# Choosing tokens in two mixture-of-experts layers: chunk maxima, one exponential, a gather from the resident activations, and weights issued earlier

## The chip, the cores and the metric

The kernel runs on one core of one Trainium2 chip. The metric is the device time of a whole execution in microseconds; the time given for a kernel is the median of its runs. One execution was taken with the hardware profiler. In its answers PE is the matmul engine (TensorE), PEld its weight loads, DVE the vector engine, ACT the scalar engine, POOL the GpSimd engine and SP the engine that issues most DMAs. Each engine works through its own instructions in order.

## The reference

Four layers act on a tensor of 4 batches, 128 channels and 64 x 64 positions: a state-space convolution, a graph convolution, and two layers of attention followed by a mixture of experts, on 4096 tokens of 128 values per batch. The change is in what follows an attention, and that is, cut to what matters:

```python
# z = layernorm(t);  t: 4 batches x 4096 tokens x 128
logits = einsum('bsd,ed->bse', z, gate_w) + gate_b       # 64 experts
probs = softmax(logits, axis=1)                           # over the 4096 tokens
vals, idx = top_k(probs.transpose(0, 2, 1), 8)            # each expert chooses 8 tokens
gathered = take(z, idx)                                   # 8 x 64 tokens of a batch
pooled = einsum('bked,bke->bed', gathered, topv)          # weighted sum of the eight
h = gelu(pooled_and_1 @ weight1)                          # 64 experts: 129 -> 512
out = h_and_1 @ weight2                                   # 513 -> 128
t = t + scatter_add(idx, out * topv)                      # back to the chosen tokens
```

An expert thus needs, for each batch, the eight largest of 4096 logits, their softmax weights, the weighted sum of the eight normed tokens, and its answer goes back to the same eight tokens with the same weights.

## The kernel before

Layers 0 and 1 run together until about 3330 us. `layer1_end` then fills `X`, a tile of 128 partitions x 4 batches x 32 blocks x 128 values, which stays on the chip: a block is 128 tokens, one per partition. `attn2`, `ffn("L2_ffn")`, `attn3` and `ffn("L3_ffn", out)` work on `X` in place.

`ffn` goes over two pairs of batches, `p` = 0 and 1; the two batches of a pair (`r` = 0, 1) take 64 partitions each, since there are 64 experts. Its steps, with the names and lines of the profile:

- *Logits.* Tokens come in 8 chunks of 512 (`c`). `ln_stats` (L700 to L712) gives mean and reciprocal deviation for 16 blocks at once: bn_stats on DVE, a square root on ACT. For each block `normed` writes the normed tile `zf` on DVE (L716), PE transposes it (L1071, `ps_t`), the four transposes are copied out (L1073, `zTf`, on ACT for r = 0 and on DVE for r = 1), and a matmul with the gate weights (L1074) gives logits in PSUM, which ACT writes with the bias to `lg` (L1077), 128 x 4096 in the end. The normed tiles of a whole pair are kept in `zs`: 17 buffers of four blocks.
- *Choice.* DVE finds the eight largest of each row of 4096 (L1081), writes a copy `ch` in which they are replaced by a very negative number (L1083), and negates the largest (L1085). ACT takes the exponential of `lg` in place, with its row sum `den` (L1087), and of `ch` (L1088). DVE subtracts the two (L1091). What is left in `lg` is the unnormalised softmax weight at the chosen tokens and zero elsewhere.
- *Gather.* For each chunk PE transposes `lg` (L1098, `ps_rt`), ACT copies it out (L1100, `rt`), and eight matmuls against the kept normed tiles sum the chosen tokens (L1104, `ps_p`). DVE divides by `den` (L1109), PE transposes (L1111), DVE writes `pooled` (L1112).
- *Experts.* Sixteen groups of four experts. `load` issues a group's two weight transfers of 1 MB each on SP's queue (L1048, L1051) and a small one on ACT's (L1053), into a pool of two buffers. Matmuls (L1126, L1128), Gelu on ACT (L1133), transposes (L1136), copy on DVE (L1138), matmuls (L1141), and after each four groups L1146 to L1150.
- *Scatter.* Matmuls of `lg` with the experts' answers (L1175), added to `X` on DVE (L1180); in the last layer the sum is transposed back as well and goes to the output (L1187 to L1196).

In attention 2 the normed tile is written by ACT in a second form, one activation with scale and bias (L776, bias from L760); the change uses this form in `ffn` too.

What order the engines follow is not the program's own. A scheduler orders the instructions of all stages by priority (about the order of the program) and by its own estimate of when each could run, and hands each engine one list. So work of a stage can stand ahead of its place: in the order before, nearly all statistics of a stage's tokens (L700) stand in the attention before it, and the first two weight groups of each `ffn` stand as soon as their buffers are free.

Of the kernel before, what the change touches and what calls it, by code (L numbers as in the profile page):

```python
# [19 lines left out]
N = 4096  # L20
CH = 512
NCH = N // CH
NB = N // P
E = 64
HF = 512
TOPK = 8


def bc(ap, n):
# [4 lines left out]
def bc_last(ap, n):  # L34

    return ap.unsqueeze(len(ap.shape)).to_broadcast([*ap.shape, n])


class Net:
# [652 lines left out]
                        (nc.vector.tensor_copy if h else nc.scalar.copy)(self.X[:, b, k : k + 4, :], pt)  # L692


    def ln_stats(self, sp, b, j0, n):

        nc, X = self.nc, self.X
        st = sp.tile([P, n, 6], F32, tag="lnst", name="lnst")
        for j in range(n):
            nc.vector.bn_stats(st[:, j, :], X[:, b, j0 + j, :])  # L700
        nm = sp.tile([P, n], F32, tag="lnnm", name="lnnm")
        rs = sp.tile([P, n], F32, tag="lnrs", name="lnrs")
        d = sp.tile([P, n], F32, tag="lnd", name="lnd")

        nc.vector.tensor_tensor(nm, st[:, :, 1], st[:, :, 4], ALU.add)
        nc.vector.tensor_tensor(d, st[:, :, 1], st[:, :, 4], ALU.subtract)
        nc.vector.tensor_tensor(rs, st[:, :, 2], st[:, :, 5], ALU.add)
# [147 lines left out]
    def attn3(self):  # L855
# [11 lines left out]
        with ExitStack() as ctx:  # L867
# [132 lines left out]
            for s in range(n + 4):  # L1000
# [8 lines left out]
                if 0 <= s - 3 < n:  # L1009
                    put(s - 3)  # L1010

    def ffn(self, name, out=None):

        nc, tc, a, X = self.nc, self.tc, self.a, self.X
        EG = 4
        NG = E // EG
        M = 32  # L1020
        with ExitStack() as ctx:
            wp = ctx.enter_context(tc.tile_pool(name="fw", bufs=1))
            big = ctx.enter_context(tc.tile_pool(name="fb", bufs=2))
            tp = ctx.enter_context(tc.tile_pool(name="ft", bufs=4))
            sp = ctx.enter_context(tc.tile_pool(name="fs", bufs=4))
            ew = ctx.enter_context(tc.tile_pool(name="fe", bufs=2))
            ps = ctx.enter_context(tc.tile_pool(name="fps", bufs=2, space=PSUM))
            aps = ctx.enter_context(tc.tile_pool(name="fa", bufs=2, space=PSUM))

            gw = wp.tile([E, P], F32, tag="gw", name="gw")  # L1030
# [11 lines left out]
            nc.vector.memset(pooled[:, E * B :], 0.0)  # L1042
            weights = []

            def load(g):
                e0 = g * EG
                w1 = ew.tile([P, EG, HF], F32, tag="w1", name="w1")
                nc.sync.dma_start(w1, a[f"{name}_weight1"][e0 : e0 + EG, 0:C, :].rearrange("e d h -> d e h"))  # L1048

                w2 = ew.tile([P, EG, 4, P], F32, tag="w2", name="w2f")  # L1050
                nc.sync.dma_start(w2, a[f"{name}_weight2"][e0 : e0 + EG, 0:HF, :].rearrange("e (p c) o -> p e c o", c=4))  # L1051
                b1 = ew.tile([EG, HF], F32, tag="b1", name="b1")
                nc.scalar.dma_start(b1, a[f"{name}_weight1"][e0 : e0 + EG, C, :])  # L1053
                return w1, w2, b1

            route, dens = [], []
            for p in range(B // 2):
                lg = big.tile([P, N], F32, tag="lg", name="lg")
                zs = [[big.tile([P, 4, P], F32, tag="z", name="zf", bufs=17) for r in range(2)] for c in range(NCH)]
                for c in range(NCH):  # L1060
                    pl = ps.tile([P, CH], F32, tag="ps", name="ps_l")
                    for r in range(2):
                        if c % 4 == 0:
                            if r == 0:
                                st = {}
                            st[r] = self.ln_stats(sp, 2 * p + r, 4 * c, 16)
                        pt = ps.tile([P, 4, P], F32, tag="tr", name="ps_t")
                        for i in range(4):
                            j = 4 * c + i
                            self.normed(zs[c][r][:, i, :], 2 * p + r, j, *st[r], j % 16)  # L1070
                            nc.tensor.transpose(pt[:, i, :], zs[c][r][:, i, :], self.ident)  # L1071
                        zT = tp.tile([P, 4, P], F32, tag="s", name="zTf")
                        (nc.vector.tensor_copy if r else nc.scalar.copy)(zT, pt)  # L1073
                        nc.tensor.matmul(  # L1074
                            pl[r * E : (r + 1) * E, :], gwT, zT.rearrange("p i c -> p (i c)"), start=True, stop=True
                        )
                    nc.scalar.activation(lg[:, c * CH : (c + 1) * CH], pl, AF.Identity, bias=gb)  # L1077


                m8 = sp.tile([P, TOPK], F32, tag="m8", name="m8")  # L1080
                nc.vector.max(m8, lg)  # L1081
                ch = wp.tile([P, N], F32, tag="ch", name="ch")
                nc.vector.match_replace(ch, m8, lg, -3.0e38)  # L1083
                nmax = sp.tile([P, 1], F32, tag="nmax", name="nmax")
                nc.vector.tensor_scalar(nmax, m8[:, 0:1], -1.0, None, ALU.mult)  # L1085
                den = sp.tile([P, 1], F32, tag="den", name="den")
                nc.scalar.activation(lg, lg, AF.Exp, bias=nmax, accum_out=den)  # L1087
                nc.scalar.activation(ch, ch, AF.Exp, bias=nmax)  # L1088
                nc.vector.reciprocal(den, den)

                nc.vector.tensor_tensor(lg, lg, ch, ALU.subtract)  # L1091
                route.append(lg)
                dens.append(den)
                pp = aps.tile([P, P], F32, tag="acc", name="ps_p")
                for c in range(NCH):
                    pt = ps.tile([P, 4, P], F32, tag="tr", name="ps_rt")
                    for i in range(4):
                        nc.tensor.transpose(pt[:, i, :], lg[:, (4 * c + i) * P : (4 * c + i + 1) * P], self.ident)  # L1098
                    rt = tp.tile([P, 4, P], F32, tag="s", name="rt")
                    nc.scalar.copy(rt, pt)  # L1100
                    for i in range(4):
                        j = 4 * c + i
                        for r in range(2):
                            nc.tensor.matmul(  # L1104
                                pp[r * E : (r + 1) * E, :], rt[:, i, r * E : (r + 1) * E], zs[c][r][:, i, :],
                                start=j == 0, stop=j == NB - 1,
                            )
                pd = tp.tile([P, P], F32, tag="s2", name="pd", bufs=3)
                nc.vector.tensor_scalar(pd, pp, den, None, ALU.mult)  # L1109
                pt = ps.tile([P, P], F32, tag="tr", name="ps_pt")  # L1110
                nc.tensor.transpose(pt, pd, self.ident)  # L1111
                nc.vector.tensor_copy(  # L1112
                    pooled[:, : E * B].rearrange("p (e b) -> p e b", b=B)[:, :, 2 * p : 2 * p + 2],
                    pt.rearrange("p (r e) -> p e r", r=2),
                )


            sel = self.sel
            outT = wp.tile([P, B, E], F32, tag="outT", name="outT")
            for q in range(NG // 4):  # L1120
                po = aps.tile([P, 4, P], F32, tag="acc", name="ps_eo")
                for k in range(4):
# [24 lines left out]
                pt = ps.tile([P, 4, P], F32, tag="tr", name="ps_oT")  # L1147
# [8 lines left out]
            for p in range(B // 2):  # L1156
                pt = ps.tile([P, P], F32, tag="tr", name="ps_ot")
# [9 lines left out]
            for p in range(B // 2):  # L1167
                for c in range(NCH):
                    for r in range(2):
                        if out is None:  # L1170

                            j = 4 * c + 2 * r
# [8 lines left out]
                        else:  # L1181

                            b = 2 * p + r
                            sl = slice(c * CH, (c + 1) * CH)
# [9 lines left out]
                            o = tp.tile([P, CH], F32, tag="s", name="of")  # L1194
# [16 lines left out]

# [47 lines left out]
```

## Time and profile before

| | us |
|---|---|
| median of three runs | 4361.5 (4350.91 to 4377.3) |
| profiled execution | 4357.93 |
| its span | 4356.1 |
| FFN 2: X final to the last logits of pair 1 | 97.3 (3661.2 to 3758.5) |
| FFN 2: from there to the first expert matmul L1128 | 38.05 |
| FFN 3: the same two stretches | 93.1 and 39.2 |
| layer1_end, attention 2, FFN 2 | 3330 to 3396, to 3661, to 3919 |
| attention 3, FFN 3 with the output | 3919 to 4066, to 4356 |

The span is what the profiler saw from the first instruction to the last; the profiled execution's own time is 1.8 us longer, and the median lies 3.6 above that. Stage bounds are rounded to a microsecond, as neighbouring stages overlap. In an answer about groups or the timeline a row gives a line, an engine and an operation with its output and inputs; a bracket holds the engine's idle time ahead of it and what ended that. Shares of busy time over the whole span (PE 82%, DVE 69%, ACT 48%) are averages over stages with different limits.

### The profile page before, as it was taken

What the parts mean: (1) busy time and instruction counts of PE and PEld (TensorE: products, weight loads), DVE (VectorE), ACT (ScalarE), POOL (GpSimd) and SP (SyncE); (2) the same over time, 40 slices, a digit from 0 to 9 for tenths busy, and PEclk for the clock granted to TensorE, in tenths of its full rate; (3) what the DMA queues carried; (4) which work ended last, traced back from release to release, by engine and by line L of the source; (5) the groups of instructions that cost most, each with busy time, mean ns of one, the idle gap of its engine ahead of it and who ended that gap; (6) DMA issues with size and microseconds to landing.
All of it is one profiled execution on the core that took longest, in us unless ns stands there. A gap on an engine that the chain in (4) does not pass through costs nothing. (4 is left out here: it accounts for less than half of the span.)

```text
span 4356.1 us, 49147 instructions
## 1 busy us (share of the span) xinstructions
PE 3553.7 (82%) x17367; PEld 1989.9 (46%) x17367; DVE 3002.4 (69%) x4815; ACT 2084.0 (48%) x3467; POOL 2463.4 (57%) x1235
## 2 busy tenths in 40 slices
PE   6877868888896888889688888989997798688768
PEld 2333333444543344554334445445654576347535
DVE  5988889897667999866699876655311776438721
ACT  4555654455544445654444555411322785308421
POOL 5999888887786988778698877820002100003100
PEclk8988978899998899999879999999997899799888
DMA  3454544555373444436445553631225100170045
GB/s 105 149 152 147 149 109 131 134 137 137 100 217 113 131 138 136 137 105 210 122 123 135 139 141 105 186 106 60 77 75 200 37 1 2 41 271 2 2 154 195
DMA packets 261991, 523.95 MB, mean 120 GB/s; under 512 B 22346, under 2 KB 24562, under 8 KB 261746
## 3 DMA queue, kind: packets, MB, share of 16 engines
q1 hardware_dynamic: 250450, 501.45, 39.2%
q10 hardware_dynamic: 11296, 19.37, 1.3%
q8 instruction: 137, 2.24, 0.2%
q14 instruction: 108, 0.88, 0.1%
HBM read 443.15 MB, written 77.59 MB: 120 GB/s over the span
## 5 line engine op out<-in xcount | busy, mean ns | idle before, releaser
L284 POOL TENSOR_TENSOR db<-dx,bt 128x1024 f32<-128x1024 f32 x512 | 1203.6, 2354 | 331.8 <-DVE hs L302 216.0
L302 DVE TENSOR_TENSOR_SCAN hs<-hs,carry,db 128x512 f32<-128x512 f32 x812 | 1035.2, 1282 | 176.0 <-ACT hs L296 93.5
L296 ACT ACTIVATE hs<-dl,A 128x512 f32<-128x512 f32 x1024 | 706.6, 692 | 744.6 <-DVE ho L312 691.0
L319 POOL TENSOR_TENSOR ho_s<-ho_s,ho 128x1024 f32<-128x1024 f32 x288 | 677.4, 2352 | 13.6 <-DVE ho L312 12.9
L497 PE MATMUL ps_g<-xn 128*128 128x512 f32 x1152 | 604.2, 655 | 98.5 <-DVE inc L500 73.1
L312 DVE TENSOR_TENSOR ho<-hs,bt 128x1024 f32<-128x1024 f32 x464 | 563.2, 1214 | 1.6
L520 PE MATMUL ps_ed<-xs,inc 128*128 128x258 f16 x4096 | 511.4, 285 | 19.5 <-DVE inc L500 8.7
L520 PEld LDWEIGHTS <-inc 128*128 128x128 fp8e4 x4096 | 416.6, 102 | 134.9 <-issue 62.1
L500 DVE SCALAR_TENSOR_TENSOR inc<-ps_g,hcl,hb 128x512 fp8e4<-128x512 f32 x576 | 420.3, 736 | 39.1 <-PE ps_g L497 23.2
L497 PEld LDWEIGHTS ps_g<-xn 128*128 128x128 f32 x1152 | 216.5, 205 | 416.3 <-DVE inc L500 182.3
L340 PE MATMUL ps_y<-ho,cst 128*128 128x512 f32 x512 | 275.1, 681 | 109.3 <-POOL ho L308 92.0
L620 PE MATMUL ps_v<-inc_v,es 128*128 128x512 fp8e4 x1536 | 342.6, 382 | 19.3 <-DVE rb L628 18.1
L620 PEld LDWEIGHTS <-es 128*128 128x128 f16 x2048 | 202.4, 99 | 288.5 <-issue 63.1
L513 ACT CAST inc<-ps_t 128x512 fp8e4<-128x512 f32 x448 | 232.1, 600 | 95.4 <-PE ps_t L509 95.3
L222 PE MATMUL ps_c<-xt,wc 128*128 128x512 f32 x512 | 234.0, 611 | 11.6 <-DVE inc L500 6.8
L340 PEld LDWEIGHTS ps_y<-ho,cst 128*128 128x128 f32 x512 | 105.5, 215 | 269.8 <-POOL ho L308 122.4
L526 ACT COPY ed<-ps_ed 128x129 f32<-128x129 f32 x128 | 34.0, 266 | 380.0 <-PE ps_ed L520 380.0
L527 DVE TENSOR_TENSOR ed<-ps_ed,ed 128x129 f32<-128x129 f32 x128 | 36.6, 286 | 211.1 <-ACT ed L526 208.1
L302 DVE TENSOR_TENSOR_SCAN hs<-hs,db 128x512 f32<-128x512 f32 x116 | 141.2, 1223 | 53.2 <-POOL db L284 42.2
L536 POOL TENSOR_TENSOR ed<-ed,rdeg 128x512 f32<-128x512 f32 x32 | 33.3, 1040 | 250.7 <-DVE rdeg L532 250.7
L222 PEld LDWEIGHTS ps_c<-xt,wc 128*128 128x128 f32 x512 | 99.2, 197 | 137.6 <-issue 116.4
L509 PE MATMUL ps_t<-ident,strip 128*128 128x128 fp8e4 x1344 | 114.8, 227 | 53.5 <-DVE ed L527 18.9
(293 smaller groups left out, 5513.2 us busy)
## 6 DMA issues: line engine op xcount, KB each, us to landing
bt<-bcd SPq DMA_DIRECT2D x512, 512.0 KB
inc<-inc SPq DMA_DIRECT2D x192, 256.0 KB
inc_v<-inc SPq DMA_DIRECT2D x96, 512.0 KB
w<-in_L_ffn_weight SPq DMA_DIRECT2D x32, 1024.0 KB
w2f<-in_L_ffn_weight SPq DMA_DIRECT2D x32, 1024.0 KB
strip<-inc SPq DMA_DIRECT2D x84, 256.0 KB
x<-x ACTq DMA_DIRECT2D x32, 256.0 KB
xn<-x SPq DMA_DIRECT2D x32, 256.0 KB
```

The costliest lines, as they stand in the source:

```text
L222: nc.tensor.matmul(s["ps"][h], wc[:, h, j, :], xt[:, j : j + T], start=j == 0, stop=j == 3)
L284: nc.gpsimd.tensor_tensor(db, s["dx"], bc(s["bt", n][:, 0, :], 2), ALU.mult)
L296: act(nc.scalar.activation(hs[:, k, :], s["dl"][:, k, :], AF.Exp, scale=A[:, k, n : n + 1]))
L302: nc.vector.tensor_tensor_scan(to[:, h, :], hs[:, h, :], db[:, h, :], init, ALU.mult, ALU.add)
L312: nc.vector.tensor_tensor(ho, hs, ct, ALU.mult)
L319: nc.gpsimd.tensor_tensor(s["sum", n // G], s["sum", n // G], ho, ALU.add)
L340: nc.tensor.matmul(s["y"][h], self.ident, t[:, h, :], start=False, stop=n == DS - 1 and k == len(terms) - 1,)
L497: nc.tensor.matmul(pq, xn[v // 4][:, v % 4 * P : (v % 4 + 1) * P], xn[c], start=True, stop=True)
L500: nc.vector.scalar_tensor_tensor(inc[:, v, :], pq, hc[:, v : v + 1], hb, ALU.subtract, ALU.is_gt, saturate=False)
L513: later(1, lambda: act(nc.scalar.copy(inc[:, v, :], pt, saturate=False)))
L520: nc.tensor.matmul(pe[:, : 2 * P + 2], inc[:, v, i * P : (i + 1) * P], xs[:, v, :], start=v == 0, stop=v == NB - 1,)
L620: nc.tensor.matmul(pv, es[:, e, k, :], inc[:, e, :], start=e == 0 and k == 0, stop=e == NB - 1 and k == 1,)
```

## The change

It changes `ffn` and what is issued ahead of it.

- The eight largest are found per chunk of 512, as its logits come (`best`, 8 x 8 per row), and then among these 64. The replacement writes -2^127. One exponential goes to a tile of its own, `ex`, and no longer to `lg`. An operation in four quarters of 1024 writes to `lg` the product of (`ch` = -2^127) and `ex`, in place of the second exponential and the subtraction.
- The normed tiles are not kept. `zf` has 8 buffers of one block; even blocks are written by DVE, odd ones by ACT. The reciprocal deviations of a pair are kept in `rsk`. The gather multiplies the transposed weights by them as it takes them out of PSUM, on DVE, sums over `X` itself, and takes off the mean with a row sum (`m`).
- The order in the program is logits(0), choose(0), logits(1), gather(0), choose(1), gather(1). The pool of two PSUM buffers has three.
- `load` becomes a method with a pool that lives for the whole kernel; groups 0 and 1 of layer 2 are issued ahead of attention 2, those of layer 3 ahead of attention 3. In the scheduled order, layer 2's now stand on SP's queue in layers 0 and 1 (near 2860 us by their neighbours), where they stood among the loads of `layer1_end`; layer 3's stand where they did.

The core of the diff; a line of "..." marks what is left out:

```diff
+TAKEN = -(2.0**127)
+EG = 4
...
-        rs = sp.tile([P, n], F32, tag="lnrs", name="lnrs")
+        if rs is None:
+            rs = sp.tile([P, n], F32, tag="lnrs", name="lnrs")
...
+    def load(self, name, g):
...
-            ew = ctx.enter_context(tc.tile_pool(name="fe", bufs=2))
-            ps = ctx.enter_context(tc.tile_pool(name="fps", bufs=2, space=PSUM))
+            ps = ctx.enter_context(tc.tile_pool(name="fps", bufs=3, space=PSUM))
...
-            def load(g):
...
+            rsk = [wp.tile([P, NB, 2], F32, tag=f"rs{p}", name="rsk") for p in range(B // 2)]
+            route, tops, dens = [], [], []
+            def logits(p):
                 lg = big.tile([P, N], F32, tag="lg", name="lg")
-                zs = [[big.tile([P, 4, P], F32, tag="z", name="zf", bufs=17) for r in range(2)] for c in range(NCH)]
+                best = sp.tile([P, NCH, TOPK], F32, tag="best", name="best")
+                st = {}
                 for c in range(NCH):
                     pl = ps.tile([P, CH], F32, tag="ps", name="ps_l")
                     for r in range(2):
                         if c % 4 == 0:
-                            if r == 0:
-                                st = {}
-                            st[r] = self.ln_stats(sp, 2 * p + r, 4 * c, 16)
+                            st[r] = self.ln_stats(sp, 2 * p + r, 4 * c, 16, rsk[p][:, 4 * c : 4 * c + 16, r])
+                            nm, rs = st[r]
+                            nb = sp.tile([P, 16], F32, tag="lnnb", name="lnnb")
+                            nc.vector.tensor_tensor(nb, nm, rs, ALU.mult)
+                            st[r] = nm, rs, nb
+                        nm, rs, nb = st[r]
                         pt = ps.tile([P, 4, P], F32, tag="tr", name="ps_t")
                         for i in range(4):
                             j = 4 * c + i
-                            self.normed(zs[c][r][:, i, :], 2 * p + r, j, *st[r], j % 16)
-                            nc.tensor.transpose(pt[:, i, :], zs[c][r][:, i, :], self.ident)
+                            z = tp.tile([P, P], F32, tag="z", name="zf", bufs=8)
+                            if i % 2:
+                                k = j % 16
+                                nc.scalar.activation(
+                                    z, X[:, 2 * p + r, j, :], AF.Identity, scale=rs[:, k : k + 1], bias=nb[:, k : k + 1]
+                                )
+                            else:
+                                self.normed(z, 2 * p + r, j, nm, rs, j % 16)
+                            nc.tensor.transpose(pt[:, i, :], z, self.ident)
                         zT = tp.tile([P, 4, P], F32, tag="s", name="zTf")
                         (nc.vector.tensor_copy if r else nc.scalar.copy)(zT, pt)
                         nc.tensor.matmul(
                             pl[r * E : (r + 1) * E, :], gwT, zT.rearrange("p i c -> p (i c)"), start=True, stop=True
                         )
                     nc.scalar.activation(lg[:, c * CH : (c + 1) * CH], pl, AF.Identity, bias=gb)
+                    nc.vector.max(best[:, c, :], lg[:, c * CH : (c + 1) * CH])
+                route.append(lg)
+                tops.append(best)
+            def choose(p):
+                lg = route[p]
                 m8 = sp.tile([P, TOPK], F32, tag="m8", name="m8")
-                nc.vector.max(m8, lg)
-                ch = wp.tile([P, N], F32, tag="ch", name="ch")
-                nc.vector.match_replace(ch, m8, lg, -3.0e38)
+                nc.vector.max(m8, tops[p].rearrange("p c k -> p (c k)"))
                 nmax = sp.tile([P, 1], F32, tag="nmax", name="nmax")
                 nc.vector.tensor_scalar(nmax, m8[:, 0:1], -1.0, None, ALU.mult)
+                ch = wp.tile([P, N], F32, tag="ch", name="ch")
+                nc.vector.match_replace(ch, m8, lg, TAKEN)
                 den = sp.tile([P, 1], F32, tag="den", name="den")
-                nc.scalar.activation(lg, lg, AF.Exp, bias=nmax, accum_out=den)
-                nc.scalar.activation(ch, ch, AF.Exp, bias=nmax)
+                ex = wp.tile([P, N], F32, tag="ex", name="exf")
+                nc.scalar.activation(ex, lg, AF.Exp, bias=nmax, accum_out=den)
+                for q in range(4):
+                    sl = slice(q * N // 4, (q + 1) * N // 4)
+                    nc.vector.scalar_tensor_tensor(lg[:, sl], ch[:, sl], TAKEN, ex[:, sl], ALU.is_equal, ALU.mult)
                 nc.vector.reciprocal(den, den)
-                nc.vector.tensor_tensor(lg, lg, ch, ALU.subtract)
-                route.append(lg)
                 dens.append(den)
+            def gather(p):
+                lg = route[p]
                 pp = aps.tile([P, P], F32, tag="acc", name="ps_p")
...
-                    nc.scalar.copy(rt, pt)
+                    nc.vector.tensor_tensor(
+                        rt.rearrange("p i (r e) -> p i r e", r=2), pt.rearrange("p i (r e) -> p i r e", r=2),
+                        bc_last(rsk[p][:, 4 * c : 4 * c + 4, :], E), ALU.mult,
+                    )
...
                             nc.tensor.matmul(
-                                pp[r * E : (r + 1) * E, :], rt[:, i, r * E : (r + 1) * E], zs[c][r][:, i, :],
+                                pp[r * E : (r + 1) * E, :], rt[:, i, r * E : (r + 1) * E], X[:, 2 * p + r, j, :],
                                 start=j == 0, stop=j == NB - 1,
                             )
+                m = sp.tile([P, 1], F32, tag="m", name="m")
+                nc.vector.reduce_sum(m, pp, axis=AX.X)
+                nc.vector.tensor_scalar(m, m, -1.0 / C, None, ALU.mult)
                 pd = tp.tile([P, P], F32, tag="s2", name="pd", bufs=3)
-                nc.vector.tensor_scalar(pd, pp, den, None, ALU.mult)
+                nc.vector.tensor_scalar(pd, pp, m, dens[p], ALU.add, ALU.mult)
                 pt = ps.tile([P, P], F32, tag="tr", name="ps_pt")
...
+            logits(0)
+            choose(0)
+            logits(1)
+            gather(0)
+            choose(1)
+            gather(1)
...
-                    w1, w2, b1 = load(g)
+                    w1, w2, b1 = self.ahead[g] if g < len(self.ahead) else self.load(name, g)
...
+    net.ew = ctx.enter_context(tc.tile_pool(name="fe", bufs=2))
     net.layer1_end()
+    net.ahead = [net.load("L2_ffn", g) for g in range(2)]
     net.attn2()
     net.ffn("L2_ffn")
+    net.ahead = [net.load("L3_ffn", g) for g in range(2)]
     net.attn3()
     net.ffn("L3_ffn", out)
```

More of the change, by code (lines that the diff above doesn't have):

```diff
@@ L692, in layer1_end, with ln_stats @@
                         (nc.vector.tensor_copy if h else nc.scalar.copy)(self.X[:, b, k : k + 4, :], pt)
-    def ln_stats(self, sp, b, j0, n):
+    def ln_stats(self, sp, b, j0, n, rs=None):
         nc, X = self.nc, self.X
@@ L1010, in attn3 @@
                     put(s - 3)
+    def load(self, name, g):
+        nc, a, ew = self.nc, self.a, self.ew
+        e0 = g * EG
+        w1 = ew.tile([P, EG, HF], F32, tag="w1", name="w1")
+        nc.sync.dma_start(w1, a[f"{name}_weight1"][e0 : e0 + EG, 0:C, :].rearrange("e d h -> d e h"))
+        w2 = ew.tile([P, EG, 4, P], F32, tag="w2", name="w2f")
+        nc.sync.dma_start(w2, a[f"{name}_weight2"][e0 : e0 + EG, 0:HF, :].rearrange("e (p c) o -> p e c o", c=4))
+        b1 = ew.tile([EG, HF], F32, tag="b1", name="b1")
+        nc.scalar.dma_start(b1, a[f"{name}_weight1"][e0 : e0 + EG, C, :])
+        return w1, w2, b1
     def ffn(self, name, out=None):
         nc, tc, a, X = self.nc, self.tc, self.a, self.X
-        EG = 4
         NG = E // EG
@@ L1043, in ffn @@
             weights = []
-            def load(g):
[L1046 to L1057, printed above, removed]
+            rsk = [wp.tile([P, NB, 2], F32, tag=f"rs{p}", name="rsk") for p in range(B // 2)]
+            route, tops, dens = [], [], []
+            def logits(p):
                 lg = big.tile([P, N], F32, tag="lg", name="lg")
-                zs = [[big.tile([P, 4, P], F32, tag="z", name="zf", bufs=17) for r in range(2)] for c in range(NCH)]
+                best = sp.tile([P, NCH, TOPK], F32, tag="best", name="best")
+                st = {}
                 for c in range(NCH):
```

## The prediction

> **What bounds the kernel now.** I read the granted clock first (mean 0.9, one core), then the slices, then the busy time stage by stage, because the change touches the two FFN stages and what is loaded for them. Stage times, in us from the span's start; columns: length, busy time of PE, weight load, DVE, ACT, POOL, granted clock, DMA share, GB/s.
>
> ```profile
> 3330.00:3396.00 66.00, 31.12 (x128) 24.93 (x128) 11.23 (x20) 29.74 (x34) 37.37 (x16) 0.53 0.78 271
> 3396.00:3661.00 265.00, 243.22 (x1652) 199.18 (x1651) 198.91 (x782) 207.42 (x446) 0.23 (x5) 0.97 0.01 2
> 3661.00:3697.00 36.00, 27.61 (x97) 11.38 (x97) 25.39 (x94) 11.79 (x20) 0.64 (x2) 0.86 0.02 3
> 3697.00:3718.00 21.00, 0.00 (x0) 0.00 (x0) 13.69 (x17) 10.27 (x6) 0.00 (x0) 0.55 0.00 0
> 3718.00:3758.00 40.00, 36.22 (x258) 22.81 (x259) 21.84 (x72) 13.69 (x24) 0.00 (x0) 0.94 0.00 1
> 3758.00:3781.00 23.00, 1.85 (x5) 0.48 (x4) 13.56 (x6) 9.18 (x5) 0.00 (x0) 0.56 0.00 1
> 3781.00:3797.00 16.00, 14.34 (x165) 12.06 (x169) 0.64 (x2) 4.39 (x8) 0.00 (x0) 0.89 0.01 2
> 3797.00:3884.00 87.00, 67.53 (x748) 31.96 (x740) 11.89 (x19) 13.07 (x21) 0.00 (x0) 0.88 0.91 340
> ```
>
> The rows are the end of layer 1, attention 2, and then FFN 2: logits of the first batch pair, its choice, gather with the second pair's logits, the second choice, gather, experts, scatter. In the two choice rows PE does nothing for 21 and 23 us; FFN 3 has two more (22 and 22 us). The experts' row is DMA's (share 0.91). The timeline gives the choice as one chain:
>
> ```profile
> 3695.77 4.43 DVE L1081 MAX8 m<-lg 128x8 f32<-128x4096 f32 x1 [0.86 <-ACT lg L1077]
> 3700.43 4.41 DVE L1083 MATCH_REPLACE8 ch<-m,lg 128x4096 f32<-128x4096 f32 x1
> 3704.98 1.28 ACT L1087 ACT_TABLE_LOAD   x1 [8.85 <-DVE nmax L1085]
> 3706.28 3.71 ACT L1087 ACTIVATE lg<-lg,nmax 128x4096 f32<-128x4096 f32 x1
> 3709.98 3.69 ACT L1088 ACTIVATE ch<-ch,nmax 128x4096 f32<-128x4096 f32 x1
> 3713.71 4.42 DVE L1091 TENSOR_TENSOR lg<-lg,ch 128x4096 f32<-128x4096 f32 x1 [3.44 <-ACT ch L1088]
> 3718.28 1.94 PE L1098 MATMUL ps_rt<-cst,lg 128*128 128x128 f32 x8 [23.26 <-DVE lg L1091]
> ```
>
> 4.43 + 4.41 + 1.28 + 3.71 + 3.69 + 4.42 = 21.9, plus hand-overs: PE stands 23.26 us. The waits of FFN 2 (waiter, releaser, total, times, longest) confirm it:
>
> ```profile
> PE ps_rt L1098 <- DVE lg L1091: 44.4, 2, 23.3
> ```
>
> In FFN 2 the last logits of pair 1 are there at 3758.5, 97.3 us after X is final (3661.2); the first expert matmul starts 38.05 us later (3796.56). In FFN 3: 93.1 and 39.2 us.
>
> [...] The trace shows 1.283 for the load, but the Exp starts 0.02 us after it[...]. [...] 0.55 in the choice row, and the first eight transposes take 1.94 us where eight at full clock take 1.09. [...]
>
> **The change, part by part** (new lines named by tile).
>
> *Logits.* Before, DVE writes all eight normed tiles of a chunk of 512 tokens and keeps them. Now DVE writes four, ACT four into eight short-lived buffers, and one maximum per chunk is added. DVE per chunk: 4 × 0.268 (L716 back to back) + one 128x512 copy 0.61 (L1073 overlapped) + maximum 0.6 (4.43/8 = 0.55 and a start; bounds 0.55 and 0.75) + about four bn_stats × 0.2 = 3.1. The bn_stats are new here: in the static order about 60 of an FFN's 128 stand in its logits phase, before nearly all were hoisted into attention. ACT: 4 × 0.40 to 0.50 (L776, the same operation, takes 0.496 alone) + copy 0.48 + lg 0.6 = 2.7 to 3.1. PE: 1.09 + 1.07 = 2.2. Before, pair 0's chunks took 3.6 us with DVE at 2.83, 79% of it. The same share of 3.1 gives 3.9; 3.3 would be DVE almost full. I take 3.8. Sixteen chunks: 60.8.
>
> *First choice.* It lies inside the logits: pair 1's follow in program order. DVE: match_replace 4.5, beside it the table load and one Exp (1.28 + 3.71 = 5.0), then four quarters of compare-and-multiply. A quarter has no row[...]. In all 4.5 + 0.6 + 4.9 = 10.0, in which PE gets only the tiles already queued.
>
> *Start.* In ACT's order five DMA issues, a Sqrt table load (1.28) and four small activations now stand ahead of its first normed tile. In FFN 2 I put the first transposes 7.2 us behind X, 4.3 in FFN 3 (the issues took to 3665.2 before); before, it was under 1.
>
> FFN 2: 7.2 + 60.8 + 10.0 = 78.0 for 97.3, −19.3. FFN 3: 75.1 for 93.1, −18.0.
>
> *Last logits to first expert matmul.* Maxima 0.75 and nmax 0.15, match_replace 4.5 (Exp hidden up to 0.6), rt of pair 0 six times between (6 × 0.69, DVE instead of ACT), four quarters 4.9: 14.5. These six rt and their matmuls are pair 0's gather, which fills PE where it stood 23 us. Then pair 1's gather: it took 3781.2 to 3796.6, 15.4 us, at the evacuation's 0.586 on ACT; at 0.69 on DVE with three PSUM buffers PE still sets it, 15.5 with the added row sum (0.3). Together 30, against 38.05 and 39.2: −8.0 and −9.2. A Gelu table load exposed before (1.28, ACT at 3797.7) is now ordered ahead; that is inside the 30.
>
> *Loads.* L2's first two groups (four of 1 MB) moved from among layer1_end's x loads to about 2860 us, behind three xn loads and ahead of the other stores and loads on SP's queue; two b1 loads move on ACT. DMA is at 0.49 in layers 0/1, and the next xn is wanted at 2887: 4.2 MB at 400 GB/s is 10.5 us, so 0 to +2, taken +1. In layer1_end DMA ran at 406 GB/s while the loads passed; tiles took 4.64 us, 3.87 after. Five tiles × 0.77 = 3.9 and a part of ACT's 7 us wait for x: −5 (bounds 0 and −13; nothing if POOL's 2.35 per tile or the rest of that pipeline takes over). L3's groups are issued where they were, behind L2's experts: 0.
>
> *Attention.* Fewer bn_stats inside it and table loads 22 to 14 in attention 2. PE holds the steady unit (7.51 us), units with loads take 8.0: four of them × 0.5 = −2 (−8 to +3). Attention 3 likewise −2.
>
> Sum: −37.3 − 17.2 − 5 − 4 + 1 = −62.5. The profiled execution took 4357.9 (span 4356.1): 4295.4. Median of the runs shown is 4361.5, 3.6 above it: 4299.
>
> **The rivals.**
> *Coupling (the other side).* Every transpose group now needs tiles of two in-order queues; a zTf or lg waiting for PE at ACT's head holds ACT's tiles, those hold the transposes, these the eight buffers DVE waits for. If each half chunk becomes a round trip, a chunk costs up to 2 × (z 0.5 + transposes 0.6 + copy 0.7 + matmul 0.55 + hand-overs 0.4) = 5.5. Break-even of an FFN: 16 × c + 17.2 − 8 = 97.3, c = 5.5; with the rest of −8 to help it is c = 5.75. At 6.2 the kernel takes about 4377. For: waits on both queues in the static order, 9.7 us ACT wait at L1073 in eight chunks already. Against: eight buffers are a whole chunk ahead, three PSUM buffers.
> *DVE becomes the bound.* With bn_stats, maxima, rt and hand-overs a chunk at 4.6: +0.8 × 32 = +26: 4325. For: DVE gains work just where it was 70% busy. Against: 3.1 summed.
> *Loading ahead is hidden or costs.* layer1_end limited by POOL and ACT, +5, and layers 0/1 +2: 4306.
> *Better overlap.* Chunks at 3.2, first choice half filled by queued work (−5 each): −19 − 10 = 4270.
> *That the choice doesn't shorten* is excluded: the removed Exp, maximum and whole-row subtract are on PE's wait itself, unless PE's filler order fails: then the tail is 38 again, 4316.
>
> **How the numbers follow.** Measurement tells about 0.5% (22 us) from no change. Forecast (with the loads' case) 0.58: 4282 to 4316. DVE bound or filler failing 0.22: 4316 to 4341. Better overlap 0.13: 4262 to 4282. Coupling 0.07: 4341 to 4390. The range, leaving out the tenth at either end: 4270 to 4336. Faster than 4340: 0.58 + 0.13 + 0.21 = 0.92; same 0.05; slower 0.03.
>
> **What would show it.** PE's wait for rt behind the choice below 12 us in the second choice, and gone as one block in the first; logits chunks at 3.8 (wrong if 4.5); last logits 78 and 75 us after X is final, the first expert matmul 30 later; granted clock in the FFN above 0.8 throughout; layer1_end at 61; experts unchanged at 87 and 99 us. Wrong if ACT's waits for ps_t and DVE's for zf's buffers grow beyond 1 us per chunk, if the experts' stage grows, or if X is final after 3661 (I expect 3655).

## The result

The changed kernel took 4333.65 us (median of seven runs, 4320.59 to 4347.82), the kernel before 4361.5 us (seven runs, 4350.91 to 4377.3). The ratio is 0.9933, 95% interval 0.9906 to 0.996: some 28 us gained, where 62.5 were forecast. The profiled execution took 4332.47 us, its span 4330.7, at a granted clock of 0.899 (0.900 before).

Stage times of the changed kernel, columns as in the prediction (length; busy time of PE, weight load, DVE, ACT, POOL; granted clock, DMA share, GB/s). The rows: end of layer 1, attention 2, FFN 2's logits of pair 0, from there to pair 1's last logits (the first choice is in it), from there to the first expert matmul, experts; then FFN 3's pair 0 and the stretch after it.

```profile
3339.00:3397.00 58.00, 29.48 (x120) 23.52 (x120) 10.37 (x15) 26.45 (x30) 37.08 (x16) 0.53 0.71 235
3397.00:3663.60 266.60, 246.65 (x1659) 201.18 (x1659) 186.43 (x704) 199.35 (x435) 0.40 (x6) 0.96 0.01 2
3669.30:3702.70 33.40, 28.72 (x103) 11.91 (x103) 25.59 (x95) 24.00 (x54) 0.00 (x0) 0.92 0.00 0
3702.70:3748.20 45.50, 32.40 (x110) 13.25 (x111) 34.82 (x95) 27.66 (x51) 0.00 (x0) 0.81 0.00 1
3748.20:3778.90 30.70, 26.20 (x316) 22.51 (x315) 21.08 (x32) 6.37 (x4) 0.00 (x0) 0.89 0.01 2
3778.90:3877.40 98.50, 77.27 (x751) 36.89 (x752) 14.43 (x28) 11.89 (x20) 0.00 (x0) 0.77 0.95 337
4055.80:4090.80 35.00, 28.01 (x99) 11.19 (x99) 26.70 (x102) 22.91 (x52) 0.00 (x0) 0.94 0.00 1
4090.80:4140.20 49.40, 35.63 (x113) 14.86 (x115) 35.72 (x98) 28.83 (x53) 0.00 (x0) 0.72 0.00 0
```

No engine is full in the logits: in pair 0 of FFN 2 DVE is in use for 25.6 of 33.4 us, ACT for 24.0. The choice itself is shorter, as its second instance shows in the timeline:

```profile
3748.17 0.69 DVE L1095 MAX8 best<-lg 128x8 f32<-128x512 f32 x1 [1.32 <-ACT lg L1094]
3748.90 0.23 DVE L1104 MAX8 m<-best 128x8 f32<-128x64 f32 x1
3749.30 4.41 DVE L1108 MATCH_REPLACE8 ch<-m,lg 128x4096 f32<-128x4096 f32 x1
3749.39 1.28 ACT L1111 ACT_TABLE_LOAD   x1 [1.25 <-DVE nmax L1106]
3750.69 3.71 ACT L1111 ACTIVATE exf<-lg,nmax 128x4096 f32<-128x4096 f32 x1
3754.36 5.39 PE L1136 MATMUL ps_p<-X,rt 128*64 128x128 f32 x48 [1.53 <-DVE rt L1129]
3755.42 3.49 DVE L1115 SCALAR_TENSOR_TENSOR lg<-ch,exf 128x1024 f32<-128x1024 f32 x3
```

Table load and Exp run beside match_replace, and pair 0's gather (L1136) fills PE. The wait of 23.26 us that carried the prediction is not among the waits of FFN 2 any more.

**Where the time went.** Executions of one kernel differ in two places that the change leaves nearly alone. The stretch up to layer1_end was between 3324.7 and 3340.9 us in all the profiles here, and an experts' stage between 90.9 and 108.5 where no work was added to it (the first experiment shows what its length goes with). Without these two, three profiles of the kernel before give 832.5, 831.2 and 830.8 us, two of the changed kernel 789.7 and 793.3: 40.0 us less. I take this for what the change does. The runs' 28 (17 to 41 by the interval) hold it together with those two, and 40 is near the end of that interval. But over the six variants below that have a ratio and leave the experts alone, the gain by the ratio less the gain outside the two places is between -8 and +12 us, and under 1 in the mean, so the runs don't show that the change costs time there. By stages, means of the same profiles:

| | before | after | change | forecast |
|---|---|---|---|---|
| layer1_end, first to last POOL add | 58.7 | 56.2 | -2.5 | -5 |
| attention 2 and 3 | 269.4, 146.6 | 268.6, 145.9 | -1.5 | -4 |
| FFN 2, X final to last logits | 95.6 | 85.8 | -9.8 | -19.3 |
| FFN 3, the same | 93.3 | 88.1 | -5.2 | -18.0 |
| last logits to first expert matmul | 38.8, 38.4 | 30.9, 30.9 | -15.4 | -17.2 |
| scatter of FFN 2, output of FFN 3 | 32.1, 58.5 | 29.0, 56.0 | -5.6 | 0 |

Of the 34 us by which the runs fell short of the forecast, 22 are one term, the logits: -15.0 where -37.3 was forecast. Most of what is left is the difference between 40 and 28.

### The profile page after: what moved, and what is told of

It is laid out like the page before. It is cut to its first block, busy times and chain, and to the rows that moved or that the text cites. A ratio compares the mean times of both kernels' runs of the same rounds, so it can differ in the third digit from the quotient of the medians.

```text
span 4330.7 us, 49179 instructions
## 1 busy us (share of the span) xinstructions
PE 3584.4 (83%) x17367; PEld 2004.0 (46%) x17367; DVE 3001.4 (69%) x4787; ACT 2094.7 (48%) x3551; POOL 2463.2 (57%) x1235
## 5 line engine op out<-in xcount | busy, mean ns | idle before, releaser
L304 DVE TENSOR_TENSOR_SCAN hs<-hs,db 128x512 f32<-128x512 f32 x116 | 141.3, 1223 | 54.3 <-POOL db L286 43.3
```

What stands on the lines that cost most here:

```text
L304: nc.vector.tensor_tensor_scan(to[:, h, :], hs[:, h, :], db[:, h, :], init, ALU.mult, ALU.add)
```

## The experiments

Ratios are to the kernel before on the same chip. "Pair 0" is from the first transpose to pair 0's last logits, "rest" from there to pair 1's, "tail" from there to the first expert matmul.

**Both kernels again.** No edit.

> The kernel before once more, for a second profile. If the clock of TensorE in the experts' stages is a matter of chance, the two stages (first expert matmul to the last ob) differ from 90.9 and 99.5 us by up to 8 us, with the time at half clock (21 and 38 us then), some 0.3 to 0.4 us for each us at half clock. If the change caused the 98.5 and 103.5 us of the kernel after, this one shows 91 and 99 again, within 2. Logits of pair 0: 34 and 31; from there to the last logits of pair 1: 63 and 62; tail 38 and 39.

> The changed kernel once more. Chance: experts' stages anywhere from 88 to 104 us, following the time at half clock. Caused by the change: 98.5 and 103.5 again within 2. The stretch up to the start of layer1_end was 5.8 us longer in its first profile, all of it gained before 1520 us, where nothing is changed: by chance it is within 6 us of 3333 again, with either sign; if the change did it, +5 to +6. Logits of pair 0: 33 and 35 with 5.7 and 3.7 of start; rest 45 and 49; tail 31.

> The kernel before a third time, for its experts' stages. Chance: FFN 2's and FFN 3's lie on the line of about 81 us + 0.4 x time at half clock, anywhere from 88 to 108, and one of the two FFN 2 stages so far (90.9, 93.9) could as well have been 100. If the change makes FFN 2's experts slower by itself, FFN 2's is 94 or less again, while the changed kernel and its variants had 95 to 107.

The kernel before had experts' stages of 93.9 and 108.5 us, and in a third profile 107.0 and 103.0; the changed one 101.8 and 107.4. So the kernel before, too, can have a long experts' stage in FFN 2, which speaks for chance and not for the change. Two executions of that one stage of the kernel before, first profile and third:

```profile
3796.60:3887.50 90.90, 69.70 (x754) 33.29 (x755) 14.44 (x28) 13.07 (x21) 0.00 (x0) 0.88 0.91 337
```

```profile
3786.80:3893.80 107.00, 86.19 (x753) 40.36 (x754) 14.44 (x28) 13.07 (x21) 0.00 (x0) 0.71 0.81 287
```

DVE's and ACT's work is the same to a hundredth; PE's is 16.5 us longer at a lower clock, and the DMA share falls with it. Over 30 experts' stages in 15 profiles (all but the variant with more PE work) the length is 86.4 us + 0.31 times the time at half clock, with a spread of 1.3 us about that line. Their mean is 100.5 in the kernel before (six) and 101.8 in the changed kernel and its variants (24).

The stretch up to layer1_end was 5.8 us longer in the changed kernel's first profile. Set side by side, POOL's instructions stand 5.7 or 5.8 us apart from 1837 us to 3333 us; the weight loads moved to 2866 add nothing to it. The step that was forecast at +1 is 0.

**Statistics left out.** Work is left out here (see the expectation).

```diff
-        for j in range(n):
+        for j in range(n if rs is None else 1):
             nc.vector.bn_stats(st[:, j, :], X[:, b, j0 + j, :])
+        if rs is not None:
+            nc.vector.tensor_copy(st[:, 1:, :], st[:, 0:1, :].to_broadcast([P, n - 1, 6]))
```

> Leaves work out: in the FFNs bn_stats runs for one block of 16 and its result is copied to the other 15; the output is not the reference's. It takes about 110 bn_stats of 0.27 us off DVE in each FFN, all else stays. If DVE's sum sets the chunks (3.2 us of 4.2 in use), pair 0's eight chunks fall from 33.4 and 35.0 to 26 to 28 us, the rest of the logits by 5 to 6 us each, the kernel by 24 us or more. If the hand-overs between the in-order queues set them, they stay within 2 us (31 to 35) and the kernel gains under 10 us, most of it in attention where some of these instructions stood.

```profile
3660.50:3693.60 33.10, 28.67 (x101) 11.40 (x101) 21.53 (x70) 23.57 (x55) 0.00 (x0) 0.93 0.00 0
3693.60:3735.90 42.30, 32.53 (x111) 12.73 (x113) 28.84 (x56) 26.43 (x49) 0.00 (x0) 0.88 0.00 1
```

DVE has 4.1 us less in pair 0, which stays at 33.1 (35.1 in FFN 3): DVE's sum doesn't set pair 0. The rest fell from 45.5 and 49.4 to 42.3 and 41.4, so there DVE's work does count. Outside layers 0/1 and the experts this variant took 775.6 us, 14 to 18 less than the changed kernel, which is between the two expectations. The ratio was 0.9891 (0.9867 to 0.9914).

Most of what the rest gained lies in one place. Statistics come for sixteen blocks, that is for four chunks, at a time. In the changed kernel those of pair 1's second half are finished only when its fifth chunk needs them:

```profile
3727.11 0.69 ACT L1094 ACTIVATE lg<-ps_l,gb 128x512 f32<-128x512 f32 x1 [0.69 <-PE ps_l L1091]
3728.94 1.44 DVE L702 BATCH_NORM_STATS2 lnst<-X 128x6 f32<-128x128 f32 x7
3731.20 0.31 ACT L714 ACTIVATE rsk<-rsk,eps 128x16 f32<-128x16 f32 x1 [0.60 <-DVE rsk L712]
3731.93 1.11 DVE L719 TENSOR_SCALAR zf<-X,lnnm,rsk 128x128 f32<-128x128 f32 x4
3736.31 0.69 ACT L1094 ACTIVATE lg<-ps_l,gb 128x512 f32<-128x512 f32 x1 [2.17 <-PE ps_l L1091]
```

The fifth chunk's logits came 9.2 us after the fourth's (8.8 in FFN 3); without the statistics it was 3.5 in both.

**All normed tiles on DVE.**

```diff
-                            if i % 2:
+                            if False:
```

> All normed tiles on DVE again, everything else as in the changed kernel. DVE gains 32 tiles x 0.31 = 10 us per pair. If DVE's sum sets the chunks, pair 0 goes from 33.4 and 35.0 to about 43 us, and the kernel is 25 to 40 us slower than the changed one. If the hand-overs between two engines that share each transpose group set them, pair 0 stays at 33 to 37 although DVE does 1.2 us more per chunk, and the kernel stays within 12 us of the changed one.

Pair 0 took 37.4 and 37.4 us, just above the second expectation, and the rest 59.6 and 62.0 us. Outside layers 0/1 and the experts it took 817.7 us, 24 to 28 more than the changed kernel, close to the first expectation; ratio 0.9983 (0.9966 to 1.0001). Sharing the tiles with ACT, as the change does, is worth 16 us per FFN against this variant, most of it in pair 1. Pair 0 of FFN 2:

```profile
3652.50:3689.90 37.40, 29.03 (x98) 11.18 (x98) 28.72 (x96) 9.56 (x18) 0.00 (x0) 0.93 0.00 0
```

ACT is nearly free here, with 9.6 us of work, and pair 0 is longer all the same: it doesn't help to take tiles off ACT if DVE, now in use for 28.7 us, gets them.

**One maximum over 4096.** The maximum of before, everything else changed.

```diff
-                    nc.vector.max(best[:, c, :], lg[:, c * CH : (c + 1) * CH])
...
-                nc.vector.max(m8, tops[p].rearrange("p c k -> p (c k)"))
+                nc.vector.max(m8, lg)
```

> The changed kernel with one maximum over 4096 logits ahead of the choice, as before, in place of the chunk maxima; all else of the change stays. Theory of the ring: the chunk maximum stands in DVE's queue waiting for ACT's lg, which waits for PE, and DVE's next tiles and copies, which PE needs, stand behind it. Then pair 0's eight chunks fall from 33.3 and 35.0 to 28 to 30 us, pair 1's likewise, which about pays the 3.7 us that each of four choices gets longer: the kernel within 8 us of the changed one. If the maxima are no link of the loop, the chunks stay within 1 us and the kernel is about 15 us slower than the changed one.

Pair 0: 32.1 and 32.5; rest 43.8 and 43.3; tail 32.5 and 32.7. The first choices took 15.1 and 15.2 us where they had 11.9 and 11.6, the tails 1.8 more; pair 0 gained 1.2 and 2.5 us and the rest more. Logits, choice and gather of both FFNs sum to 226.3 us against 234.3 and 237.1. The chunk maxima are thus no gain here but a loss of 8 to 11 us, which neither expectation had. The loop through them can explain at most the 1.2 and 2.5 us of pair 0, not the 3 to 7 expected. In pair 1 a second thing changed: the scheduler put more of the bn_stats into pair 0 (10 and 16 are left in the rest, of 23 and 25), and the fifth chunk took 1.3 and 3.7 us. What part of the gain is the maxima's own isn't shown. The ratio was 0.9879 (0.9851 to 0.9907).

**The order of before.**

```diff
-            logits(1)
             gather(0)
+            logits(1)
```

> The changed kernel with the program order of before: gather of pair 0 ahead of pair 1's logits. My account: the tail (last logits to first expert matmul) gets shorter by the six rt between, 30.8 to 26 or 27, but the 13 us of gather now lie among pair 1's logits: rest 47 and 49 to 57 to 60; the kernel 10 to 16 us slower than the changed one. Rival: gather fills PE's gaps among pair 1's logits[...]: rest up by under 5, the kernel the same or faster.

Rest 57.2 and 57.9, tail 27.0 and 27.2: both inside my account's numbers. Logits, choice and gather sum to 246.9, 10 to 13 us more than in the changed kernel, so by the stages of one profile the new order is worth that. The runs don't show it: the ratio is 0.9903 (0.9876 to 0.9929), and its interval overlaps with that of the changed kernel's 0.9933.

**The loads where they were.** The pool goes back into the FFN, and nothing is issued ahead.

```diff
+            self.ew = ctx.enter_context(tc.tile_pool(name="fe", bufs=2))
...
-    net.ew = ctx.enter_context(tc.tile_pool(name="fe", bufs=2))
+    net.ahead = []
```

> The changed kernel with the weights' pool inside each FFN again and no early issue. If the loads were worth what I forecast, layer1_end is 5 us longer than the changed kernel's 56; by the two profiles it should be 2 to 3 longer (58.6). The time up to layer1_end differs only by chance. If layer 3's loads, which now run at the end of layer 2's experts, slow those, the experts' stage of FFN 2 is 91 to 95 here against 98 to 102; if the clock's chance does it, its length follows the time at half clock on the same line (about 81 + 0.4 x that time).

layer1_end took 58.0 us, against 55.9 and 56.6 in the changed kernel. But in the ten other variants, which all have the loads ahead, it took 54.4 to 57.7; the mean of these twelve profiles is 56.8. So the loads' place is worth some 1 us, not clear of that spread. The experts took 104.7 and 102.7, at 52 and 55 us of half clock: without layer 3's loads at its end, layer 2's experts' stage was no shorter.

**Two PSUM buffers.**

```diff
-            ps = ctx.enter_context(tc.tile_pool(name="fps", bufs=3, space=PSUM))
+            ps = ctx.enter_context(tc.tile_pool(name="fps", bufs=2, space=PSUM))
```

> The changed kernel with two PSUM buffers of each kind in place of three. If the third one gave the 2.9 and 2.6 us that scatter and output gained, they are 31.8 and 58.6 again. Pair 0's chunks: if hand-overs limit them, a buffer less makes them longer, 35 to 40 us; if it is the ring through the maxima alone, unchanged. Tail: gather alternates in groups of two, 31 to 34.

Scatter 32.0, output 57.1, pair 0 36.5 and 36.3, tail 33.3 and 34.1, rest 43.4 and 49.3; outside layers 0/1 and experts 801.3 us, 8 to 12 more. The third buffer, which I had costed at nothing outside the gather, is thus about a quarter of the 40 us. The scatter's gain went wholly with it. Of the output's 2.5 us only 1.1 went, and variants with three buffers took 56.0 to 57.9 there, so what shortened the output isn't shown.

**One normed tile in four on POOL.** First with one maximum (its edit is above) and the five small gate loads on SP's queue (one of three lines is shown), then these parted.

```diff
-                nc.scalar.dma_start(gb[r * E : (r + 1) * E, :], a[f"{name}_gate_b"])
+                nc.sync.dma_start(gb[r * E : (r + 1) * E, :], a[f"{name}_gate_b"])
...
+                            if i == 3:
+                                nc.gpsimd.tensor_scalar(
+                                    z, X[:, 2 * p + r, j, :], nm[:, j % 16 : j % 16 + 1], rs[:, j % 16 : j % 16 + 1], ALU.add, ALU.mult
+                                )
-                            if i % 2:
+                            elif i % 2:
```

> An attempt at a better kernel: the changed one with one maximum over 4096, the small gate loads on SP's queue in place of ACT's, and every fourth normed tile on POOL in place of ACT (POOL is idle here; its operation on 128 values has no row, 0.4 to 0.6 us by L969's 0.73 for 256). If hand-overs with a long ACT queue limit the chunks, pair 0 falls from 32.1 and 32.5 to 27 to 29 and the start from 5.7 and 3.7 to under 3; the kernel is at a ratio of 0.983 to before or below. If POOL's tile comes late in each group, pair 0 is at 33 to 36 and the ratio stays near 0.988.

> The changed kernel with one maximum over 4096 and the small gate loads on SP's queue; no tile on POOL. It parts the gain of the attempt before: if the loads gave the start and POOL the chunks, the start is 3.4 and 1.8 here and pair 0 stays at 31 to 33; if the early start itself freed the chunks, pair 0 is at 25 to 27 already.

> The changed kernel with its chunk maxima, every fourth normed tile on POOL in place of ACT, nothing else. If ACT's queue (four tiles, a copy and a row of logits per chunk, 3.0 of 4.2 us) is what makes PE wait, pair 0 falls from 33.3 and 35.0 to 26 to 29 although the maxima stay. If the loop through the maxima is needed for it, pair 0 stays at 31 to 34 and only both together reach 25.

| | start | pair 0 | rest | tail |
|---|---|---|---|---|
| changed kernel | 5.7, 3.7 | 33.4, 35.0 | 45.5, 49.4 | 30.7, 30.9 |
| one maximum, loads on SP | 3.3, 1.8 | 31.3, 31.5 | 43.2, 44.2 | 32.7, 32.5 |
| tile on POOL alone | 5.7, 3.7 | 27.2, 29.2 | 47.6, 50.2 | 30.8, 29.8 |
| all three | 3.4, 1.8 | 25.2, 25.6 | 44.4, 44.5 | 32.5, 33.5 |

Pair 0 of FFN 2 with only the tile moved, the chunk maxima in place:

```profile
3670.60:3697.80 27.20, 25.02 (x100) 11.40 (x100) 21.36 (x71) 16.11 (x35) 7.20 (x17) 0.92 0.00 0
```

ACT has 16.1 us where it had 24.0, and pair 0 is 6 us shorter in both FFNs, with the maxima still there. DVE has 4.2 us less as well, since the scheduler left only 11 bn_stats in this stretch, of 24. But the variant without statistics had the same DVE work, 21.5 us, with ACT at 23.6, and took 33.1. Set side by side, these two leave ACT's share of the tiles as what made the difference (FFN 3: DVE 22.8 and 21.8, ACT 23.5 and 15.7, pair 0 35.1 and 29.2). Whether the third queue helps by itself, apart from ACT's smaller load, isn't parted. In the changed kernel ACT's 33.4 us were its 24.0 us of work and waits, the largest of them this one, for logits that PE had not made yet; ACT's next tiles stand behind each:

```profile
ACT lg L1094 <- PE ps_l L1091: 6.4, 7, 1.7
```

All three together, DVE 19.45 of 25.2, are the best kernel found: 4308.9 us, ratio 0.9856 (0.9819 to 0.9892), logits, choice and gather 210.9 us in its profile. Pair 0 is better than expected, the start not under 3. The interval doesn't overlap with that of the changed kernel's 0.9933. The wait of pair 1's fifth chunk is still in it, 8.2 and 6.6 us.

**The clock in the first choice.** On top of the last kernel:

```diff
+                if p == 0:
+                    pw = aps.tile([P, CH], F32, tag="acc", name="ps_w")
+                    for k in range(16):
+                        nc.tensor.matmul(
+                            pw, self.ident, lg[:, N - CH :] if k < 8 else ch[:, :CH], start=True, stop=True,
+                        )
```

> The attempt with POOL, and 16 matmuls more in the first choice, whose result nobody reads: eight when the last logits of pair 0 are there, eight after match_replace, so that PE is busy for most of the choice. Nothing is left out. If the half clock that the choice leaves behind (20.5 of the 44.4 us up to pair 1's last logits) slows pair 1's logits, the time at half clock falls under 8 us and the stretch to 37 to 40; the kernel gains 8 to 14 us. If pair 1 waits for DVE (36.9 us in use of 44.4), the clock rises and the stretch stays at 43 to 46.

```profile
3685.90:3730.10 44.20, 37.62 (x139) 17.83 (x141) 36.82 (x107) 23.15 (x38) 7.19 (x15) 0.92 0.00 1
```

The time at half clock fell from 20.5 to 6.8 us; the stretch stayed (44.2 and 45.4 for 44.4 and 44.5), with DVE in use for 36.8. Some 9 us of it had been in the choice itself (clock 0.69 over 14.7 us), where PE has next to nothing to do. Behind the choice the clock rose from 0.81 to 0.88, and pair 1's chunks took 29.5 us for 29.7. So the half clock that went had cost that kernel nothing; what the 6.8 us still there cost is not tested. The tail was 2 to 3 us longer; ratio 0.9867 (0.9831 to 0.9903), no gain.

**More PE work in the experts.**

```diff
+                        if c in (1, 3):
+                            nc.tensor.matmul(
+                                pw, self.ident, X[:, 0, 0:4, :].rearrange("p i c -> p (i c)"), start=True, stop=True,
+                            )
```

> The changed kernel with two matmuls of 512 columns more per expert group, whose result nobody reads: PE is busier by 1.07 us of the 5.1 us that a group's weights take. It adds work and leaves none out. If gaps in PE's work set off the half clock, its time in the experts' stages falls from 46 to 61 us to under 25, and they take 88 to 94 us. If the clock drops for another reason, each group at half clock takes 2.1 us more: 105 to 120 us.

```profile
3778.80:3900.50 121.70, 109.68 (x816) 44.59 (x817) 14.43 (x28) 11.89 (x20) 0.00 (x0) 0.82 0.78 272
```

121.7 and 119.5 us, with 45 and 39 us at half clock; ratio 1.0003 (0.9985 to 1.0022). I had mis-sized the load: each of these matmuls is two instructions, in this stage 64 for the 32 of the program and 40.1 us of PE, and not 17. PE was busy for 90% of the stage and the clock fell as before. So filling PE to that extent doesn't keep the clock. And the stage isn't DMA's alone, as I had read its share of 0.91: 40 us of PE work made it some 20 us longer, and DMA's share fell to 0.78. What sets the clock's falls off stays open.

## Why the prediction was wrong

**Logits: the step that failed is "sixteen chunks: 60.8".** With start and choice it gave 78.0 and 75.1 us from X to the last logits of pair 1; the first profile has 84.6 and 88.1. Two things were wrong with it.

*The pace of a running stretch was taken for the whole.* The 3.6 us a chunk of the kernel before are the mean of the seven chunks behind pair 0's first. That first one took 7.3 and 7.2 us there from its first transpose to its logits, and all eight 34.4 and 30.7. In the changed kernel the first chunk takes 7.4 and 7.0 us, with no other chunk to overlap with and PE at half clock (two matmuls took 1.97 us at a granted clock of 0.50, later 1.07 at 1.00), and the sum has nothing for this. The other seven follow at 3.7 and 4.0, near the 3.8. In pair 1 the fifth chunk takes 9.2 and 8.8, waiting for statistics; the sum had bn_stats as DVE's work per chunk and put the wait for them at nothing. What was over the sum, in us for FFN 2 and FFN 3: first chunk +3.6 and +3.2, the other seven of pair 0 -0.6 and +1.4, the choice +1.9 and +1.6, pair 1 behind the choice +3.2 and +7.4, start -1.5 and -0.6; together +6.6 and +13.0.

*What sets the pace was wrong too, and that 3.8 came out near 3.7 and 4.0 is luck.* I divided DVE's sum (3.1) by the 79% that DVE reached before. DVE's sum was right (25.6 us for eight chunks are 3.2 each), but the 79% isn't a property of DVE. Without the statistics DVE was in use for 65% of pair 0, and the seven chunks came at the same 3.7 and 4.0. With as little DVE work and a third of ACT's gone they came at 3.1 and 3.4. ACT's sum, 2.7 to 3.1 by my own count, was as large as DVE's, and a transpose group needs tiles of both. The rival called coupling named this, with its price set too high (5.5). The chunk maxima, costed at 0.6 each, took 0.69, and the kernel without them was faster.

**The first choice, 10.0: 11.9 and 11.6.** In FFN 2 1.9 us pass before match_replace, from 3702.66 to 3704.58, since the last maxima and nmax stand behind a copy and a tile on DVE.

**Pair 1's chunks behind it.** DVE's work counts here (statistics left out: the rest is 3 to 8 us shorter), mostly through the fifth chunk. What ACT's work counts for isn't shown: with the tile on POOL the rest took 47.6 and 50.2 us, but 13 and 19 bn_stats more stood in it. The clock has a part that I can bound only: two executions of the changed kernel had a rest of 45.5 us with 17.1 at half clock and of 48.0 with 23.9.

**The tail, 30: right,** 30.7 to 31.0, and with it the shape of the choice: six rt between, four quarters (1.217 us each; the 4.9 put into the sum for all four rested on no trace; a quarter of the 4.42 us that the kernel before took at L1091 over 4096 is 1.105), gather that fills PE. The variant with the old order gave the 26 to 27 that this account asked for.

**Start, 7.2 and 4.3: 5.7 and 3.7,** from the DMA issues on ACT as I had put it; on SP's queue they leave 3.3 and 1.8.

**Loads, -5: half of it or less,** -2.5 between the means of before and after, some 1 by the experiment. The rest of that pipeline took over, which the bounds named: POOL, in use for 37.1 of the 58.0 us, waited for ACT's o for 21.4 us, before for 23.6. That layer 3's loads were issued where they were was right for their place in the queue, but not in time: 3863 to 3873 us, before 3883 to 3885. The first now stands 13.9 us ahead of the end of FFN 2's experts, where it stood 4.6. That the pool now outlives FFN 2 may be the reason, which no run shows; no gain from it is seen.

**Attention, -4: -1.5.** In attention 2 DVE has 12.5 us less to do and ACT 8, but PE is in use for 246.7 of its 266.6 us.

**Not in the sum:** scatter and output, -5.6. The scatter's 3.1 are the third PSUM buffer's; I had named the pool's change only for the gather.

**Experts "unchanged at 87 and 99":** right as to the change, wrong as a number. That stage varies by 18 us between executions of one kernel, nearly half of the 40 that the change gives.

**The signs.** PE's wait for rt behind the choice went as forecast. ACT's waits for ps_t (2.9 us in pair 0 of FFN 2) and DVE's for zf's buffers (none) stayed under 1 us a chunk: the coupling showed elsewhere, in ACT's wait for ps_l. The granted clock was not above 0.8 throughout the FFN, but 0.72 to 0.94. X was final at 3663.6 and not at 3655, mostly since the stretch up to layer1_end was 5.8 us longer in this profile.

## What to carry to other kernels

Where no engine is full in a stage, divide the work by what each group waits for, and not by the share of the busiest engine: here ACT, with 72% in use, held the pace and DVE, with 77%, did not, and the proof was to take work off one engine at a time. See also what else such an edit moves, since a scheduler that reorders shifts other work with it. A pace measured in the middle of a stretch leaves out the first chunk and single long waits; add them apart. An operation moved ahead "as the data come" stands in an in-order queue before work that others need; here it did not pay (logits, choice and gather 234.3 and 237.1 us with the chunk maxima, 226.3 without). Before reading a difference of 1% in the total, take two profiles of the same kernel and subtract the stages that differ between them.

## What the runs showed of the hardware

In the experts' stage the granted clock fell to half for stretches of 3 to 58 us (3.4 to 34.1 in the first profiles of the two kernels), at other places in each execution, and the stage took 0.31 us more for each us of it (90.9 to 108.5 us). It did so with PE busy for 77% of a stage and for 90%. POOL's tensor_scalar on 128x128 took 0.481 us, ACT's activation on the same tile 0.486, DVE's tensor_scalar 0.335. A maximum over 512 took 0.694 us where one over 4096 takes 4.43, so eight of them are 25% dearer than one. An operation that waits holds up those behind it on its engine: in pair 0 of the changed kernel DVE stood idle for 0.70 us until ACT's lg let a chunk maximum start at 3698.03 us, and two bn_stats of X, final since 3663.6, ran behind it at 3699.40.
